# Two-layer graph network, one core: the second pass of layer 0 by lists for 16 blocks, more dense rounds and all own logits in layer 1, and row statistics by a sum and a square

## The chip, the cores and the metric

The kernel runs on one core of a Trainium2 chip. The metric is the device time of one execution in microseconds (us). All arithmetic on data is in float32.

The names of the engines in the profile: PE is TensorE (matrix products; PEld its weight loads), DVE is VectorE, ACT is ScalarE, POOL is GpSimd (here it issues the gathers), SP is SyncE (here it issues plain loads and stores). A letter q after a name is that engine's queue.

## The reference, cut to what matters

There are 3327 nodes with 512 features, and a sparse adjacency matrix with weights (some 0.3% of the entries, thick towards the first nodes, the "hubs", thin at the end, and with a full diagonal).

```
h  = relu(layernorm(x))
x  = x + adj @ (relu(adj @ (h @ W1) + b1) @ W2) + b2          # layer 0, hidden width 128

h  = relu(layernorm(x))                                       # layer 1
t  = adj @ h
attn_a = sigmoid([t, h] @ Wa.T + ba);  attn_b = sigmoid([t, h] @ Wb.T + bb)
scores[i, j] = s_left[i] + s_right[j]        # s_left, s_right: h @ W_sa times two halves of a_sa
e  = where(adj != 0, exp(-leaky_relu(scores, 0.01)), 0)
x_a = (e / (sum_j e + 1e-5)) @ (h @ W_sa)
x_b = t @ W_gcnb + b_gcnb
x  = x + sigmoid(attn_a * x_a + attn_b * x_b)
```

The layernorm has no weights; it divides by sqrt(variance + 1e-5).

## The kernel before

Nodes are padded to 3328 = 26 blocks of 128. The adjacency is given transposed, `adjT`. A *round* for a block of columns adds 128 (or two times 64) rows of some table, weighted by a piece of `adjT`. A round is *dense* where the rows are those of a known block, and goes *by list* where they are only the rows with an entry: for each group of 32 columns a list of rows is made in the kernel, and GpSimd gathers rows by it. `list_rooms` says how many list rounds of 64 rows a block's groups may take; if a group has more, a flag (`overflow`) sends the kernel through a full dense branch at its end.

**First pass of layer 0** (lines 540 to 595). Rows are normalized and multiplied with W1 (`u`), and all 26 blocks are summed densely for seven chunks of columns (`back`: 512 wide from the end, and one of 256), PE products L568. Beside it DVE takes the largest absolute value of each group (L572), from which `make_lists` makes the lists (`row_h`: node rows, `row_a`: adjacency pieces). GpSimd gathers the listed adjacency pieces into `ae` (`gather_adj`, L166), from the last blocks to the first; `gather_behind` takes one at a time and lets it wait for a product (`pace`). `load_own` loads a block's own diagonal pieces for blocks in `OWN`, whose first round is dense: the block itself, and so takes entries off the lists. Each chunk ends in `make_g`, whose rows go to `g_dram`.

**Second pass of layer 0** (L803 to L860). The chunks at the end, `LISTED = 2` of them (blocks 18 to 25), are summed by lists: `gather_g` gathers rows of g (24 in flight), `list_sums` adds them in small products (L784), one step for each block and a last one for the chunk's copy, and `gather_g` goes on as sums free its tiles. `SUMS` says beside which product a step stands. The other 18 blocks are `dense_chunks`, five rounds of 26 products (L825), whose loads go on SP's queue. Beside these, `make_h1` makes a chunk's rows: it loads x, adds b2 (L650), multiplies with W2 (px, L663), adds (L666), normalizes (`ln_relu`: bn_stats L234, bn_aggr L236, square root L238, Relu L244), scores the row (L623) and stores x and h. For a block outside `OWN` and `LATE` it also makes the row's *own logits* (`own_logits`, L630: the part `h @ Wa[d:]`, `h @ Wb[d:]` of the two attentions). `make_e_hub` and `add_hubs` do layer 1's first block, the hub, whose sums over all rows are dense (L709), as soon as rows are there. `next_late`, `next(hubs)` and `make_e_hub` are called from the loop over the products; the order on each engine is the order of these calls.

**Layer 1** (L903 to L1110). For the blocks 25 down to 1: `attend` gathers h rows by the list (or loads the block's own row into `h_own`), makes e in the other half of `ae`, and, for blocks in `OWN`, the own logits; `sums` multiplies (L981), `turn` transposes the sums (L995, copies L1010), `weigh` multiplies with W_gcnb and W_sa (L1035, L1042), `finish` makes the output. `segments` cuts a block's rounds into pieces of at most four. The three `LATE` blocks get their own logits at the beginning of the stage. `LEAD` and `pace` keep gathers three or four blocks ahead; `AE_PER = 2` adjacency pieces are gathered for each block.

## Time and profile before

| what | us |
|---|---|
| median of 14 executions | 838.49 (833.1 to 846.14) |
| the profiled execution | 841.48 |
| its span (first to last instruction) | 839.7 |
| PE busy | 744.0 (89%) |
| DVE busy | 507.2 (60%) |
| POOL busy | 460.8 (55%) |
| ACT busy | 194.4 (23%) |
| mean granted clock of PE | 0.937 |

How to read it: a busy time is a sum over a whole span in which different things bind in different stages, so shares by stage say more. The end of a matrix product is modelled in the trace, so a busy PE is not a PE at its peak. The granted clock is the share of full speed that PE was given. A gather shows as DMA_INDIRECT on POOL, and its idle time before is given with what ended it.

### The profile page before, as it was taken

How to read it: one execution, taken by the hardware profiler on the slowest of the kernel's cores; microseconds unless marked ns; L12 is line 12 of the kernel's file. 1: busy time of each engine (PE TensorE's matmuls, PEld its weight loads, DVE VectorE, ACT ScalarE, POOL GpSimd, SP SyncE). 2: the span in 40 equal slices, each digit the busy share in tenths (PEclk: the TensorE clock that was granted, in tenths of full speed). 3: DMA queues.
4: the chain of work that ended last, by engine and by line, in shares of the span. 5: the costliest groups of instructions: out<-in, count | busy, mean ns of one | idle time of the engine just before them, and what ended most of it. 6: DMA issues, size and time to landing. Idle time of an engine off the chain costs nothing.

```text
span 839.7 us, 11907 instructions
## 1 busy us (share of the span) xinstructions
PE 744.0 (89%) x3595; PEld 405.6 (48%) x3595; DVE 507.2 (60%) x1625; ACT 194.4 (23%) x402; POOL 460.8 (55%) x490
## 2 busy tenths in 40 slices
PE   9999799999897759698997759967999999999995
PEld 7774344344543324243463235643665655654454
DVE  7778868898760607788965134523666457453552
ACT  7770000000000105244542002211222222121112
POOL 2201756666557677525563766674556666767400
PEclk9999989999999769799998869986999999999999
DMA  8788989898696838789953755564668877767510
GB/s 274 241 287 262 332 242 282 249 278 276 186 290 220 276 98 307 224 275 319 330 179 114 238 139 155 181 192 122 193 200 249 252 212 222 236 204 230 171 51 29
DMA packets 104889, 185.08 MB, mean 220 GB/s; under 512 B 18401, under 2 KB 35441, under 8 KB 104818
## 3 DMA queue, kind: packets, MB, share of 16 engines
q1 hardware_dynamic: 66544, 113.43, 41.6%
q0 software_dynamic: 23264, 57.64, 24.8%
q10 hardware_dynamic: 15010, 13.18, 4.8%
q8 instruction: 30, 0.49, 0.2%
q14 instruction: 41, 0.34, 0.1%
HBM read 162.29 MB, written 22.26 MB: 220 GB/s over the span
## 4 chain that ended last, share of the span: by engine, by line
PE 74%; DVE 8%; issue 7%; DMA 4%; another core or an unknown queue 4%; ACT 1%; SPq 1%; POOL 0%; DVEq 0%; POOLq 0%; ACTq 0%
PE acc_u L568 15%; PE acc L981 13%; PE p_b L1035 12%; PE p_a L1042 11%; PE acc_g L825 8%; DMA xb<-in_x_dram 3%; PE pu L333 3%; PE ptt L995 3%; PE acc_hub L709 2%; DVE most L572 2%; PE px L663 2%; PE acc_s L784 1%; PE pt L325 1%; PE p_list L513 1%
## 5 line engine op out<-in xcount | busy, mean ns | idle before, releaser
L166 POOL DMA_INDIRECT ae<-in_adjT_dram,row_a x194 | 200.6, 1034 | 176.9 <-DVE past L519 54.2
L568 PE MATMUL acc_u<-a,rows 128*128 128x512 f32 (+1 forms) x364 | 162.7, 586 | 1.2 <-issue 1.0
L166 POOL DMA_INDIRECT hr<-h_rows,row_h x120 | 123.3, 1028 | 63.4 <-issue 28.4
L825 PE MATMUL acc_g<-a,g 128*128 128x512 f32 (+1 forms) x260 | 116.9, 584 | 9.2 <-DMA a<-in_adjT_dram 8.1
L572 DVE TENSOR_REDUCE most<-a 128x16 f32<-128x512 f32 (+1 forms) x182 | 112.7, 642 | 12.8 <-DMA a<-in_adjT_dram 8.7
L1035 PE MATMUL p_b<-W_g_sb,tyT 128*128 128x257 f32 x416 | 100.2, 393 | 14.6 <-DVE tyT L1010 13.7
L166 POOL DMA_INDIRECT rows<-h_rows,row_h x74 | 76.0, 1027 | 52.0 <-PE acc L981 21.4
L1035 PEld LDWEIGHTS p_b<-W_g_sb,tyT 128*128 128x128 f32 x416 | 78.2, 193 | 45.8 <-DVE tyT L1010 14.0
L568 PEld LDWEIGHTS acc_u<-a,rows 128*128 128x128 f32 x364 | 67.4, 197 | 60.5 <-issue 55.8
L1042 PE MATMUL p_a<-W_sa_sb,tyT 128*128 128x512 f32 (+2 forms) x216 | 93.5, 576 | 0.0
L1010 DVE COPY tyT<-ptt 128x512 f32<-128x512 f32 x51 | 34.8, 685 | 80.7 <-PE ptt L995 28.0
L825 PEld LDWEIGHTS acc_g<-a,g 128*128 128x128 f32 x260 | 50.4, 201 | 62.9 <-issue 49.8
L981 PE MATMUL acc<-hr,ae 64*64 64x512 f32 x480 | 69.3, 619 | 5.4 <-issue 4.9
L166 POOL DMA_INDIRECT g_row<-g_rows,row_h x48 | 49.2, 1025 | 23.7 <-issue 13.1
L1042 PEld LDWEIGHTS p_a<-W_sa_sb,tyT 128*128 128x128 f32 x216 | 40.9, 189 | 37.7 <-issue 35.9
L884 ACT ACTIVATE f<-f 128x2 f32<-128x2 f32 x26 | 5.3, 203 | 192.1 <-DVE f L883 98.1
L981 PEld LDWEIGHTS acc<-hr,ae 64*64 64x64 f32 x480 | 27.3, 138 | 36.8 <-issue 36.6
L343 ACT ACTIVATE gT<-acc_u,b_col 128x512 f32<-128x512 f32 (+1 forms) x7 | 4.6, 656 | 163.6 <-DMA a<-in_adjT_dram 91.3
L666 DVE TENSOR_TENSOR xb<-px,xb 128x512 f32<-128x512 f32 x26 | 17.3, 685 | 40.2 <-PE acc_g L825 21.4
L981 PE MATMUL acc<-rows,ae 64*64 64x512 f32 x296 | 39.3, 610 | 2.5 <-DVE ae L251 1.9
L623 DVE SCALAR_TENSOR_TENSOR junk<-rows,w_rows 128x512 bf16<-128x512 f32 x52 | 35.7, 687 | 6.3 <-ACT rows L244 3.1
L663 PE MATMUL px<-W_sb,sT 128*128 128x512 f32 x52 | 26.5, 643 | 13.3 <-issue 9.3
(159 smaller groups left out, 950.8 us busy)
## 6 DMA issues: line engine op xcount, KB each, us to landing
a<-in_adjT_dram SPq DMA_DIRECT2D x286, 256.0 KB
h_rows<-rows SPq DMA_DIRECT2D x26, 260.0 KB
x<-in_x_dram SPq DMA_DIRECT2D x26, 256.0 KB
xb<-in_x_dram SPq DMA_DIRECT2D x26, 256.0 KB
x<-xb ACTq DMA_DIRECT2D x26, 256.0 KB
x1b<-x SPq DMA_DIRECT2D x26, 256.0 KB
out_dram<-va SPq DMA_DIRECT2D x25, 256.0 KB
ae<-in_adjT_dram,row_a POOLq DMA_INDIRECT x194
```

Source lines behind the costliest of these rows:

```text
L166: return nc.gpsimd.indirect_dma_start(out=dst, out_offset=None, in_=table, in_offset=bass.IndirectOffsetOnAxis(ap=rows, axis=0), bounds_ch ...
L333: nc.tensor.matmul(pu[:, :HID], hT[:, k, :], W1_sb[:, k, :], start=(k == 0), stop=(k == KD - 1))
L568: added = nc.tensor.matmul(acc[:, :w], u[j], a[:, :w], start=(j == 0), stop=(j == NB - 1))
L572: nc.vector.tensor_reduce(most[:, : w // GW, j], a[:, :w].rearrange("p (b i) -> p b i", i=GW), axis=AX.X, op=ALU.max, apply_absolute_value ...
L623: return nc.vector.scalar_tensor_tensor(junk, h, 1.0, w_rows[:, s, :], op0=ALU.mult, op1=ALU.mult, accum_out=into)
L663: last_row[2] = nc.tensor.matmul(px, sT[:, b * P : (b + 1) * P], W2_sb, start=True, stop=True)
L825: added = nc.tensor.matmul(acc[:, :w], g[j], a[:, n % per, :], start=(n == 0), stop=(n == NB - 1))
L981: added = nc.tensor.matmul(taken[i]["acc"][h][q * HALF : (q + 1) * HALF, :], both[half_p, q * n + k, :], taken[i][k0][k][half_p, q, :D], s ...
L995: moved = nc.tensor.transpose(pt[:, k * P : (k + 1) * P], ty[h][:, k * P : (k + 1) * P], ident)
L1010: last = nc.vector.tensor_copy(dst, src)
L1035: nc.tensor.matmul(p_b[n][:, :WH], tyT[:, k, 0, :], W_g_sb[:, k, n * WH : (n + 1) * WH], start=(k == 0), stop=(k == KD - 1),)
L1042: last = nc.tensor.matmul(p_a[:, c0:c1], tyT[:, k, 1, :], W_sa_sb[:, k, c0:c1], start=(k == 0), stop=(k == KD - 1),)
```

## The change

- `LISTED` is 4: blocks 10 to 25 go by lists in the second pass; the dense chunks are 512, 512 and 256 columns wide. Gathers of g rows are thus 92 instead of 48.
- A tuple `TOP` of nine blocks gets a second dense round: rows 0 to 63 (for both halves of the block's columns), in layer 0 from `g_top`, in layer 1 from `h_top`. `OWN` now holds 19 blocks. `extra` is 0, 1 or 2, `list_rooms` is smaller (88 rooms in place of 97), and lists of `TOP` blocks leave out rows 0 to 63.
- The second pass is a loop over the three dense chunks, in which `SUMS` stand beside the second, and then a *free loop* of 35 turns without dense products. Its turns call list sums (`FREE_SUMS`), adjacency gathers (`FREE_AE`, behind the last g gather in GpSimd's order, and without `pace`), `next_late`, `add_behind` (a hub step if over five rows wait) and `make_e_hub`.
- All own logits are made in `attend`, from an own row that is loaded for every block; `w_own` and `bab_row` are loaded on SP's queue after layer 0; `LATE` is gone.
- `segments` leaves five rounds in one piece.
- In the second pass the addition of px also sums the row (`accum_out`), and ScalarE sums the squares of the centred row, in place of bn_stats and bn_aggr. The first pass keeps them.

The diff, cut to its core:

```diff
-LISTED = 2
+LISTED = 4
...
-LATE = 10, 11, 16
-OWN = 1, 6, 7, 8, 12, 13, 14, 15, 17, 18
+TOP = 2, 3, 4, 5, 9, 10, 11, 21, 24
+OWN = TOP + (1, 6, 7, 8, 12, 13, 14, 15, 17, 18)
 def list_rooms(n_blocks):
-    rooms = [0, 8, 7, 6, 5, 5] + 6 * [4]
-    return (rooms + n_blocks * [3])[:n_blocks]
+    rooms = [0, 8, 6, 5, 4, 4, 4, 4, 4] + n_blocks * [3]
+    rooms[21] = rooms[24] = 2
+    return rooms[:n_blocks]
...
-    extra = [int(i in OWN) for i in range(NB)]
+    extra = [int(i in OWN) + int(i in TOP) for i in range(NB)]
...
         r = rooms[i] + extra[i]
-        n = -(-r // SEG)
+        n = -(-r // SEG) - (r == SEG + 1)
...
+    def ln_relu_by_sum(dst, src, ln):
+        nc.vector.tensor_scalar(ln[:, 1:2], ln[:, 0:1], -1.0 / D, None, op0=ALU.mult)
+        nc.scalar.activation(dst, src, AF.Square, bias=ln[:, 1:2], accum_out=ln[:, 2:3])
+        nc.scalar.activation(ln[:, 3:4], ln[:, 2:3], AF.Sqrt, bias=eps, scale=1.0 / D)
+        nc.vector.reciprocal(ln[:, 4:5], ln[:, 3:4])
+        nc.vector.tensor_tensor(ln[:, 0:1], ln[:, 1:2], ln[:, 4:5], ALU.mult)
+        return nc.scalar.activation(dst, src, AF.Relu, bias=ln[:, 0:1], scale=ln[:, 4:5])
...
                 own = flag[:, groups, c0 // P + b]
                 nc.vector.tensor_tensor(own, own, apart, ALU.mult)
+                if extra[c0 // P + b] > 1:
+                    nc.vector.memset(flag[:HALF, groups, 0:1], 0.0)
...
-                    nc.vector.tensor_tensor(x1, px, x1, ALU.add)
+                    ln = l0w.tile([P, 5], F32, tag="ln5", name=f"ln_b{i}", bufs=3)
+                    nc.vector.scalar_tensor_tensor(
+                        x1, px, 1.0, x1, op0=ALU.mult, op1=ALU.add, accum_out=ln[:, 0:1]
+                    )
                     nc.scalar.dma_start(x1_dram[i], x1)
                     h = made_row(i)
-                    _, last_row[0] = ln_relu(h[:, :D], x1, l0w, f"b{i}")
+                    last_row[0] = ln_relu_by_sum(h[:, :D], x1, ln)
...
-                if not extra[i] and i not in LATE:
-                    own_logits(
-                        i, made_row(i),
-                        l0w.tile([P, D], BF16, tag="junk", name=f"junk_{i}", bufs=1),
-                    )
...
-                late.append(make_h1((c0, w), sT, False))
+                late.append(make_h1((c0, w), sT, c0 == ND))
...
-        SUMS = {1: (14, 16, 18, 20, 24), 2: (16, 18, 20, 22, 25)}
+        SUMS = 14, 16, 18, 20, 24
+        FREE_SUMS = 4, 5, 6, 7, 8, 18, 19, 20, 21, 22, 30, 31, 32, 33, 34
+        FREE_AE = {8: 6, 22: 6} | {n: 1 + n % 2 for n in range(23, 35)}
+        def add_behind():
+            if len(rows_made) - len(e_added) > 5:
+                next(hubs)
+        g_top = ae[1][:, : HID // GW, GW:]
+        for h in range(2):
+            nc.scalar.dma_start(
+                g_top[h * HALF : (h + 1) * HALF],
+                g_dram[:HALF, :].rearrange("j (k f) -> j k f", f=GW),
+            )
...
-                if n in SUMS.get(c, ()):
+                if c == 1 and n in SUMS:
                     next(summing)
-                elif c and n % 4:
-                    gather_behind(added)
-                if n % 2 or (c in (2, 3) and n % 4 == 2):
-                    with queued(last_e[0] if last and n < 8 else None):
-                        next_late()
-                if last and n >= NB - QUIET:
-                    continue
+                if n % per == per - 1 and n // per % 2:
+                    next_late()
                 if c > 1 and n % 3 == 2:
-                    next(hubs)
-                elif c > 1 and (n > 8 if last else n % 3 == 1):
-                    with queued(last_row[0] if last else None):
-                        make_e_hub()
+                    add_behind()
+                elif c > 1 and n % 3 == 1:
+                    make_e_hub()
...
+        for n in range(FREE_SUMS[-1] + 1):
+            if n in FREE_SUMS:
+                next(summing)
+            with queued(g_last[0]):
+                for _ in range(FREE_AE.get(n, 0)):
+                    next(columns)
+            next_late()
+            add_behind()
+            make_e_hub()
+        with queued(last_e[0]):
+            nc.scalar.activation(root, eps, AF.Sqrt)
         while late:
             next_late()
...
+    w_own = late_w.tile([P, 2, D], F32, tag="w_own", name="w_own")
+    nc.sync.dma_start(w_own, w_self.partition_broadcast(P))
...
+            if k0 == 0:
+                h_own = own_row(i)
             for k in range(n):
                 if k0 + k < extra[i]:
-                    h = spw.tile([P, ROW], F32, tag="h_own", name=f"h_own_{i}", bufs=3)
-                    nc.sync.dma_start(h, h_dram[i * P : (i + 1) * P, :])
+                    h = h_top if k else h_own
...
             if k0:
                 last = nc.vector.tensor_tensor(es, es, part, ALU.add)
-            elif extra[i]:
-                own_logits(i, hr[0][:, 0, :], spw.tile([P, D], BF16, tag="junk", name=f"junk_{i}"))
+            else:
+                own_of(i, h_own)
...
-        own_of(LATE[0], made[0])
+        own_of(0, own_row(0))
```

## The prediction

> **What bounds it now.** I read the slices first, then the groups by shape, then a table of busy time by stage, then the single instructions on GpSimd's queue, and last the chain. The slices show three stretches: TensorE (PE) near 9 up to slice 10 (first pass over the adjacency), broken digits from slice 11 to 23 (second pass), 9 from slice 28 on (layer 1).
>
> ```profile
> PE   9999799999897759698997759967999999999995
> DVE  7778868898760607788965134523666457453552
> POOL 2201756666557677525563766674556666767400
> PEclk9999989999999769799998869986999999999999
> ```
>
> The busy time by stage says the same in numbers. The stretches are the first dense round of the second pass (231 to 260 us), the second round (260 to 320), the third (320 to 374), the fourth (374 to 416), the fifth and narrow one (416 to 445), the last rows and the hub's end (445 to 474), the turn to layer 1 (474 to 494), and of layer 1 two pieces. Columns: PE, weight loads, DVE, ACT, POOL, granted clock, DMA share, GB/s.
>
> ```profile
> 231.00:260.00 29.00, 25.94 (x100) 11.38 (x98) 13.08 (x43) 0.47 (x1) 18.24 (x18) 1.00 0.94 309
> 260.00:320.00 60.00, 42.24 (x163) 16.94 (x164) 20.55 (x67) 8.92 (x20) 41.14 (x41) 0.77 0.58 174
> 320.00:374.00 54.00, 46.74 (x203) 20.79 (x203) 41.95 (x137) 20.18 (x36) 28.87 (x27) 0.91 0.84 273
> 374.00:416.00 42.00, 38.57 (x95) 17.12 (x94) 36.88 (x122) 21.28 (x34) 20.37 (x20) 1.00 0.97 323
> 416.00:445.00 29.00, 22.59 (x81) 14.62 (x81) 17.49 (x59) 11.15 (x21) 18.34 (x18) 0.98 0.57 181
> 445.00:474.00 29.00, 26.26 (x60) 11.43 (x64) 13.74 (x50) 6.65 (x17) 13.81 (x14) 0.91 0.62 209
> 474.00:494.00 20.00, 6.26 (x35) 2.65 (x28) 3.34 (x9) 1.70 (x4) 13.24 (x14) 0.60 0.47 128
> 556.00:580.00 24.00, 12.30 (x37) 4.98 (x36) 3.39 (x15) 1.64 (x4) 13.84 (x14) 0.58 0.50 136
> 580.00:700.00 120.00, 119.59 (x688) 72.64 (x684) 69.80 (x241) 28.80 (x62) 75.94 (x75) 1.00 0.74 217
> ```
>
> So layer 1 is PE's (119.6 of 120 us), and the second pass is nobody's: PE, DVE and DMA take turns, held together by waits. The chain that ended last names PE throughout, but with issue, DMA and unknown releasers of the second pass between:
>
> ```profile
> PE 74%; DVE 8%; issue 7%; DMA 4%; another core or an unknown queue 4%; ACT 1%; SPq 1%; POOL 0%; DVEq 0%; POOLq 0%; ACTq 0%
> ```
>
> Work taken out there moves the end only as far as the next chain allows. The likely next chain is GpSimd's queue, and its pace is in single instructions: 1.00 us each and 0.30 us to the next, so 1.30 us a gather.
>
> ```profile
> 257.77 1.00 POOL L166 DMA_INDIRECT g_row<-g_rows,row_h  x1 [0.30 <-issue]
> 259.07 1.00 POOL L166 DMA_INDIRECT g_row<-g_rows,row_h  x1 [0.30 <-issue]
> 260.37 0.99 POOL L166 DMA_INDIRECT g_row<-g_rows,row_h  x1 [0.30 <-issue]
> ```
>
> **The change, part by part.** *Lists for 16 blocks.* Two of the dense rounds go (columns 1280 to 2303): 2 x 26 products of two instructions, 104 x 0.43 us (the spacing: 40 in 17.4 us) = 45 us of PE, and 52 loads of 256 KB = 13.6 MB, 44 us at the 309 GB/s of the first round. The sums of blocks 10 to 17 by lists come in: 8 blocks of 4 or 5 rounds, 8 instructions each, in tiles that overlap (30 in 1.0 us): 9 us at most. Gathers of g rows rise from 48 to 92. The room table falls from 97 to 88 rooms, so gathers of adjacency pieces and of h rows fall from 194 to 176 each; all gathers together go from 436 to 444. I counted the non-empty rows of each group of 32 columns in the reference's inputs: no block exceeds its new room, so the fallback branch stays shut.
>
> When does layer 0 end? I follow the gathers. (a) Up to the second round's end (319.9 us, its copy out of PSUM) the order is the same but for 13 adjacency gathers fewer; I take 316 (305 to 322). (b) The third round has 256 columns: 52 products at 0.235 us (14 in 3.29 us) = 12.2, and three px pairs (2.6) and some hub products: 16 us, 332. (c) Four turns of the free loop, 2 us each (half a row on DVE, below): the sums of blocks 18 to 21 start at 340. (d) Each sum frees the rows for the next gathers. Still to come are 22 for blocks 14 to 17, 6 adjacency gathers, 24 for blocks 10 to 13 (46 of the 92 were issued in (a), two of them for block 14): 52 x 1.30 = 67.6, and 2.3 us for the last to land (572.8 issued, 574.9 landed, elsewhere in this trace): 410. (e) From the last sum to the turned sT took 4.4 us (368.3 to 372.7): 414.5. (f) The last rows: 445.4 to the last h store at 454.7 is 9.3 us for two rows; now four, and a further one costs DVE 0.77 + 0.46 + 0.77 = 2.0 us before its store: 13.3, so 428. (g) From the last h store to layer 1's first product took 19.0 us (473.7). w_own's 512 KB and the first own logits (1.5 us of DVE before the turn's copies) stand in that path now (1.7 us at 309 GB/s, and 1.5): 22 (19 to 25), so 450 against 473.7. **Layer 0 gives 23.7 us.** DVE and PE lie beside this: between 340 and 410 PE has some 50 us of work (35 hub pairs and 13 px pairs at 0.86, 9 of sums); DVE has 13 rows at 4.45 = 58 us. If this cover fails, the second pass is bound by DVE at about the same place.
>
> *Means by the addition, variances by ScalarE.* A second-pass row loses bn_stats and its aggregation (0.684 + 0.166) on DVE and gains an accumulator read (0.08, the row of the scores) and one small operation (0.15): 0.62 us less. ACT gains one 128x512 pass, which no row shows in this form; Relu of the same shape is 0.806, a copy 0.58, so between these and 1.0 with a read. The latency of a row stays (0.69 + 0.17 against 0.08 + 0.15 + 0.8), so this is worth nothing on the gathers' chain and 26 x 0.62 = 16 us where DVE bounds. DVE per row is then 0.69 + 0.77 + 0.46 + 2 x 0.77 + 4 x 0.287 = 4.6, or 4.45 where accumulator reads overlap.
>
> ```profile
> L234 DVE BATCH_NORM_STATS2 bn_b<-xb 128x6 f32<-128x512 f32 x26 | 17.0, 684 | 0.1
> L244 ACT ACTIVATE rows<-xb,ln_b 128x512 f32<-128x512 f32 x26 | 20.2, 806 | 9.1 <-PE acc_hub L709 5.6 <-DVE ln_b L240 2.1 <-issue 1.3
> L238 ACT ACT_TABLE_LOAD x8 | 10.3, 1283 | 21.6 <-DVE ln_b L236 16.7 <-DMA x<-xb 3.5 <-issue 1.4
> ```
>
> The table loads are few (8 and 10) and last 1.28 us. [...]
>
> *Own logits in layer 1.* 13 blocks' pairs (2 x 0.77 + 0.16 = 1.7 us) leave DVE's second pass (22 us, worth nothing on the gathers' chain) and go to layer 1, whose DVE is at 69.8 of 120 us: 1.7 us more in a turn of some 11 us. Blocks 17 to 12 have them there already, and PE has no idle time in those turns. Nothing, then; without that cover 13 x 1.7 = 22 us. The row that they read comes by 15 or so more loads of 260 KB on SP, at a DMA share of 0.74. The 36 more loads of own pieces (16 KB) are on ACT's queue, which has nothing else at the chunks' ends.
>
> *More dense rounds.* Rooms and extra rounds together go from 107 to 116. A fourth round lengthens PE's part of a turn from 2.63 to 3.49 us (22 against 30 products in the chain), 0.87 us: 9 x 0.87 = **7.8 us more** in layer 1, all on the path. POOL has 216 gathers there now (120 + 74 of h rows, 22 of adjacency) and 222 then (176, and the 46 that some 100 in the first pass and 30 in the free loop leave): nothing.
>
> Sum: 839.7 - 23.7 + 7.8 = 823.8 of span, with 1.8 around it 825.6. The profiled execution (841.5) is 3.0 above the median, so 838.5 - 15.9 = 822.6; I say **823**, for the case itself 811 to 835.
>
> **Rivals.** *The gaps close too* (797). PE lost 13.7 us at 474 to 494 and 11.7 at 556 to 580, both in half clock. The sum keeps them. If shifted gathers break them up, and the free loop starts at 325, it is 823 - 25 - 1 = 797. Against: the order of these gathers is hardly changed.
>
> *GpSimd's unbroken runs stop PE* (862, slower). Wherever POOL issued gathers without a break for over 13 us, PE stood or crawled until the run's end: 242 to 272 (PE's gap 270 to 278), 290 to 313 (297 to 316), 430 to 444 (439 to 446), 462 to 489 (479 to 493), 543 to 574 (556 to 577). It lost 12 to 14 us in each of 23 to 31. The free loop makes runs of 28 (36 us) and, as the later adjacency gathers no longer wait for a product, of up to 48 (62 us). If PE loses 16 of the first, the second starts 8 later; 30 of the second delay the last sums by 31: 823 + 39 = 862. It decides once the last sums come 16 us after 410. Against: runs of 8 between 580 and 740 leave PE at 1.00 clock, and POOL may merely have run on while PE waited for something else.
>
> *Nothing gained* (839). The free loop has no dense products to bridge waits. Its PE work of some 50 us at the clock of 474 to 494 (0.60) needs 83, which puts the last sums at 423 or later and the rest slower: +16. [...]
>
> *Lists overflow*: then everything is done again, beyond 1,500 us; the count above excludes it.
>
> **How the numbers follow.** Forecast 0.46, gaps close 0.24, nothing gained 0.12, runs stop PE 0.18. A measurement here tells 0.3% (2.5 us) from no change. Faster takes the first two and a third of the third: 0.74; same 0.08; slower 0.18. The range leaves out half of the slow case and the far part of the fast one: 796 to 848.
>
> **What would show it.** Right: the products of acc_g fall from 260 to 156 instructions; h's last store near 428, first product of layer 1 near 450; GpSimd at 1.30 us without long pauses between 340 and 410; layer 1 longer by 8. Wrong: PE digits of 5 or less with clock 0.5 through the free loop while POOL is unbroken; ACT_TABLE_LOAD in the dozens; gaps before the tyT copies in layer 1 where own logits precede them.

## The result and the profile after

The kernel after takes 905.4 us (median of 10) where the kernel before takes 840.4 (47 runs): 1.076 times as long, interval 1.071 to 1.080. The forecast was 823, in a range of 796 to 848. The profiled execution took 907.9 us, with a span of 906.2. Ratios, here and below, compare only executions in the faster of two states that a kernel's executions show, so they can differ a little from the quotient of the medians.

The slices of after, for comparison with those of before: PE, VectorE, GpSimd, and the clock granted to PE.

```profile
PE   9999989888878788674656628996999989999995
DVE  7779788887613245142426515652665563646643
POOL 3203666666670623676730474675766776765500
PEclk9999999999997889576766959995999999999999
```

Between slices 16 and 23, counted from 0 (362 to 544 us), PE is at 2 to 7 with a clock of 5 to 9, while POOL is mostly at 6 or 7. That comes near the sign that the prediction named for "wrong" (PE digits of 5 or less at half clock, POOL unbroken). The table by stage (us, PE, weight loads, DVE, ACT, POOL, clock, DMA share, GB/s): first dense round, second, third, then the free loop and the last rows in pieces.

```profile
231.00:275.00 44.00, 32.17 (x106) 12.46 (x104) 14.24 (x46) 0.47 (x1) 28.93 (x28) 0.88 0.72 208
275.00:326.00 51.00, 40.17 (x171) 17.88 (x171) 15.01 (x54) 12.13 (x28) 20.29 (x20) 0.83 0.74 233
326.00:347.00 21.00, 21.00 (x71) 14.13 (x72) 15.05 (x58) 11.14 (x24) 0.00 (x0) 0.92 0.73 242
347.00:380.00 33.00, 21.54 (x135) 9.15 (x134) 5.54 (x21) 8.11 (x15) 20.02 (x20) 0.70 0.32 86
380.00:415.00 35.00, 27.46 (x156) 12.37 (x155) 15.45 (x60) 11.96 (x25) 25.71 (x25) 0.74 0.48 134
415.00:445.00 30.00, 15.52 (x68) 6.86 (x66) 12.46 (x48) 12.05 (x25) 21.58 (x22) 0.78 0.43 127
445.00:475.00 30.00, 16.52 (x120) 7.42 (x119) 5.28 (x21) 3.47 (x8) 13.93 (x14) 0.59 0.13 34
```

Nobody is busy throughout from 347 on: PE at 52 to 78% (at a clock of 0.59 to 0.78, which stretches its busy time: in before the large matmuls follow 0.43 us apart at a clock of 1.00, from 240.7 to 258.1 us, and 0.85 apart at 0.50, from 278 to 283), DVE at 17 to 44%, the DMA nearly empty at the end (0.13). What PE waits for in that stretch stands in its groups between 347 and 472 us (out<-in, partitions x elements, count | busy, mean ns | idle before and what ended it):

```profile
L784 PE MATMUL acc_s<-g_row,ae 64*32 64x128 f32 x280 | 26.5, 332 | 19.3 <-issue 17.0 <-DMA g_row<-g_rows,row_h 1.0 <-DMA ae<-in_adjT_dram,row_a 0.9
L784 PE MATMUL acc_s<-g,ae 64*32 64x128 f32 x72 | 9.4, 348 | 7.0 <-issue 6.9
```

"issue" is time in which the engine waited for nothing that the profile shows. The second group needs no gathered row at all, and idles like the first. The single instructions around 364 us show how it goes: PE's list sums come in bursts 0.7 or 1.4 us apart, beside gathers that follow at 1.30 us.

```profile
363.61 0.37 PE L784 MATMUL acc_s<-g,ae 64*32 64x128 f32 x1 [0.78 <-issue]
363.63 0.62 PE L784 MATMUL acc_s<-ae,ae 64*32 64x128 f32 x3
365.07 0.69 PE L784 MATMUL acc_s<-ae,ae 64*32 64x128 f32 x5 [0.82 <-issue]
```

GpSimd's queue in the same microseconds:

```profile
362.81 1.00 POOL L164 DMA_INDIRECT g_row<-g_rows,row_h  x1 [0.30 <-issue]
364.11 1.00 POOL L164 DMA_INDIRECT g_row<-g_rows,row_h  x1 [0.30 <-issue]
365.41 0.99 POOL L164 DMA_INDIRECT g_row<-g_rows,row_h  x1 [0.30 <-issue]
```

By events, before and after: first dense round's copy out of PSUM 260.1 and 275.5, second 319.9 and 325.8; the third ends at 346.9; last list sum 472; last h store 454.7 and 506.0; layer 1's first product 473.7 and 525.2; end 839.7 and 906.2. So 51.5 us are lost ahead of layer 1 and 15.0 in it. The theory to test was the prediction's rival that unbroken runs of gathers stop PE; I call a stretch like the one above a **crawl**.

The trace of before has one too, beside the run of gathers from 290 to 313 us that the prediction names for this rival: there PE's list sums stand in the same steps of 1.4 us.

```profile
300.14 0.53 PE L784 MATMUL acc_s<-g_row,ae 64*32 64x128 f32 x4 [1.01 <-issue]
301.56 1.10 PE L784 MATMUL acc_s<-g_row,ae 64*32 64x128 f32 x4 [0.90 <-issue]
```

But the prediction's "wherever" goes too far: beside the 13 gathers from 316 to 334 us PE was busy for 17.9 of 18 us, at a clock of 0.96.

### The profile page after: what moved, and what is told of

Its sections match the earlier page's. It is cut to its first block, busy times and chain, and to the rows that moved or that the text cites. A ratio compares the mean times of both kernels' runs of the same rounds, so it can differ in the third digit from the quotient of the medians.

```text
span 906.2 us, 12320 instructions
## 1 busy us (share of the span) xinstructions
PE 757.7 (84%) x3815; PEld 411.8 (45%) x3815; DVE 491.6 (54%) x1637; ACT 211.5 (23%) x449; POOL 473.7 (52%) x507
## 4 chain that ended last, share of the span: by engine, by line
PE 67%; issue 18%; POOL 6%; DMA 3%; DVE 3%; ACT 2%; POOLq 0%; another core or an unknown queue 0%; SPq 0%; DVEq 0%; ACTq 0%
PE acc_u L579 15%; PE acc L1020 13%; PE p_b L1074 11%; PE p_a L1081 10%; POOL g_row L164 4%; PE acc_g L836 4%; PE ptt L1034 3%; PE pu L340 3%; DMA a<-in_adjT_dram 2%; PE px L665 2%; PE acc_hub L709 1%; PE acc_s L784 1%; PE pt L332 1%; PE p_list L524 1%; POOL ae L164 1%
## 5 line engine op out<-in xcount | busy, mean ns | idle before, releaser
L164 POOL DMA_INDIRECT ae<-in_adjT_dram,row_a x176 | 183.6, 1043 | 128.3 <-DVE past L530 53.5
L164 POOL DMA_INDIRECT hr<-h_rows,row_h x112 | 115.0, 1027 | 58.9 <-issue 28.5
L164 POOL DMA_INDIRECT g_row<-g_rows,row_h x92 | 95.1, 1033 | 91.2 <-PE acc_s L784 53.9
L1074 PE MATMUL p_b<-W_g_sb,tyT 128*128 128x257 f32 x416 | 104.3, 400 | 19.7 <-issue 18.6
L583 DVE TENSOR_REDUCE most<-a 128x16 f32<-128x512 f32 (+1 forms) x182 | 113.2, 643 | 13.3 <-DMA a<-in_adjT_dram 8.8
L164 POOL DMA_INDIRECT rows<-h_rows,row_h x64 | 67.6, 1056 | 88.4 <-DVE e_hub L258 46.3
L669 DVE SCALAR_TENSOR_TENSOR xb<-px,xb 128x512 f32<-128x512 f32 x26 | 17.9, 691 | 105.6 <-PE px L665 64.8
L836 PE MATMUL acc_g<-a,g 128*128 128x512 f32 (+1 forms) x156 | 67.5, 570 | 5.4 <-DMA a<-in_adjT_dram 3.9
L1020 PE MATMUL acc<-hr,ae 64*64 64x512 f32 x448 | 59.9, 607 | 1.9 <-issue 1.6
L1081 PEld LDWEIGHTS p_a<-W_sa_sb,tyT 128*128 128x128 f32 x216 | 41.1, 191 | 39.5 <-issue 36.1
L784 PE MATMUL acc_s<-g_row,ae 64*32 64x128 f32 x368 | 32.9, 325 | 23.9 <-issue 21.6
L836 PEld LDWEIGHTS acc_g<-a,g 128*128 128x128 f32 x156 | 30.0, 202 | 34.1 <-issue 22.5
L665 PE MATMUL px<-W_sb,sT 128*128 128x512 f32 x52 | 36.0, 829 | 11.3 <-ACT sT L854 6.1
```

What stands on the lines that cost most here:

```text
L164: return nc.gpsimd.indirect_dma_start(out=dst, out_offset=None, in_=table, in_offset=bass.IndirectOffsetOnAxis(ap=rows, axis=0), bounds_ch ...
L583: nc.vector.tensor_reduce(most[:, : w // GW, j], a[:, :w].rearrange("p (b i) -> p b i", i=GW), axis=AX.X, op=ALU.max, apply_absolute_value ...
L665: last_row[2] = nc.tensor.matmul(px, sT[:, b * P : (b + 1) * P], W2_sb, start=True, stop=True)
L784: nc.tensor.matmul(acc[part, b * P : (b + 1) * P], ae[i][half_p, 2 * k0 + q * (k1 - k0) + kk - k0, :GW], t[half_p, :], start=(kk == 0), st ...
L836: nc.tensor.matmul(acc[:, :w], g[j], a[:, n % per, :], start=(n == 0), stop=(n == NB - 1))
L1020: added = nc.tensor.matmul(taken[i]["acc"][h][q * HALF : (q + 1) * HALF, :], both[half_p, q * n + k, :], taken[i][k0][k][half_p, q, :D], s ...
```

## The experiments

Of six chips drawn for the experiments, two gave the kernel before 734 to 735 us and four 825 to 839, near the 838 to 840 of the case's own runs. Each result below is given beside the kernel before on its own chip.

**1. The free loop without GpSimd** (chip: before 830.6).

```
+    by_sync = [False]           # True from the start of the free loop to its last stored row
     def gather(dst, table, rows, last):
+        if by_sync[0]:
+            return nc.sync.dma_start(dst, table[:P, :])
         return nc.gpsimd.indirect_dma_start(
...
```

> The kernel after, but the gathers of the free loop (g rows and adjacency pieces) are plain loads of 128 fixed rows on SP's queue: the wrong rows, and no work for GpSimd between the third dense round's end and the last row. Its sums are wrong, the instructions on TensorE, VectorE and ScalarE the same. Theory 'runs stop TensorE': the last list sum, 465 us in the profile of after, comes near 405 (third round's end 347, then some 50 us of TensorE work), layer 1's first product near 460 instead of 525, the whole near 845. Rival 'the free loop is short of work that can run, TensorE waits for rows and sums': last sum no earlier than 450, the whole within 890 to 905.

Measured: 826.1 us, 0.996 of before (0.992 to 1.000). Last list sum at 402.5, layer 1's first product at 455.1. The prediction had 410 and 450 for these two in a loop in which gathers cost PE nothing. The table by stage shows PE at work throughout:

```profile
347.00:380.00 33.00, 32.44 (x298) 16.57 (x297) 19.70 (x72) 20.33 (x39) 2.00 (x2) 1.00 0.56 173
380.00:400.00 20.00, 17.23 (x101) 7.54 (x103) 15.12 (x59) 16.25 (x30) 0.00 (x0) 0.91 0.69 199
```

49.7 us of PE in 53, against 21.5 of 33 in the same window of after. With GpSimd's gathers, layer 1's first product came 70 us later (525.2, on another chip). This doesn't say yet whether they cost that by their pace or by holding PE up; experiment 14 divides it.

**2. The rows' statistics alone, put into before** (same chip). The new function and the addition's sum, nothing else of the change.

> The kernel before with the means from the addition and the variances by ScalarE's squares, nothing else. Theory 'worth nothing': within 0.5% of before (840), since the second pass is not VectorE's. Rival 'it saves VectorE's 16 us where rows bound (320 to 416 us)': 826 to 834. Rival 'ScalarE's square lengthens each row's chain (0.8 us and table loads of 1.28 us)': 846 or more.

Measured: 842.5, 1.019 of before (1.013 to 1.024): slower by 1.3 to 2.4%, as the second rival had it. Experiment 12 takes this up again.

**3. After without the second extra dense round** (same chip).

```
-TOP = 2, 3, 4, 5, 9, 10, 11, 21, 24
+TOP = ()
...
-    rooms = [0, 8, 6, 5, 4, 4, 4, 4, 4] + n_blocks * [3]
-    rooms[21] = rooms[24] = 2
-    return rooms[:n_blocks]
+    rooms = [0, 8, 7, 6, 5, 5] + 6 * [4]
+    return (rooms + n_blocks * [3])[:n_blocks]
```

> The kernel after with the room table of before and one dense round for the ten blocks that had one: 97 rooms and 10 extra rounds instead of 88 and 28. Theory of the prediction (0.87 us on TensorE for each of nine rounds in layer 1): 8 us less in layer 1, and some gathers more (194 instead of 176 of adjacency pieces) in the second pass; by 'runs stop TensorE' these cost up to 10 us there, so 895 to 908 in all. Rival 'the extra dense rounds are what made the change slow' (their list flags and own pieces in the first dense round, their products in layer 1): below 875.

Measured: 931.2, 1.122 of before (1.116 to 1.128). Neither theory: without them it is slower by 4% (after is at 1.076, on another chip). Layer 1 takes 411.8 us instead of 381.0. From 15 us ahead of the last h store on, GpSimd has 257 gathers to make instead of 221: 131 adjacency pieces are fetched ahead of that in both, so the longer lists leave 18 pieces and 18 row gathers more for layer 1. In layer 1 GpSimd then makes five unbroken runs of 20 to 26 gathers, where after makes one (24, at 595 us). That these runs bring the loss by crawls is likely and not shown.

**4. Products beside gathers, first attempt** (same chip). A kernel of PE products and gathers alone.

> This kernel leaves the whole computation out. TensorE runs twelve stretches of 200 steps without a wait between them: six with one 128x512 f32 product a step (0.86 us as in the kernel before), six with four products of 64 rows, 32 columns of weights and 128 elements. At step 40 of each stretch another engine starts 32 pieces of work: gathers of 128 B pieces, of 512 B rows, of 2 KB rows, of 512 B rows with a memset of 256 elements between any two, GpSimd memsets of 512 elements without a gather, and 32 plain loads of 256 KB on SP's queue. Theory 'runs stop TensorE': in the three stretches with unbroken gathers at 1.30 us the spacing of products rises from 0.86 us to 1.4 or more from about the tenth gather on, and comes back within 3 us of the last; with memsets between the gathers it stays nearer 0.86, and with memsets alone or SP's loads it is 0.86. Rival 'GpSimd merely ran on while TensorE waited': 0.86 in all six, and one spacing in the six short ones.

Measured: most gathers didn't stay in their stretches but were issued ahead, back to back, in the first 320 us. There PE made 24 or 25 matmuls in 10 us beside gathers of 128 B pieces (10 to 38 us), and 4 to 6 beside gathers of longer rows (40 to 90). That looked like a matter of size, and a refill of PE's instructions (16 KB, each 256 instructions, on a DMA queue of its own) lay at 39.3 us. So the next kernel held the gathers in place and tried both.

**5. Size, refill and breaks** (chip: before 839.1).

> This kernel leaves the whole computation out. TensorE runs 12 stretches of 192 128x512 f32 products (four instructions each) without a wait; in each, GpSimd starts one row of work, in its order: 40 unbroken gathers of 128 B pieces, of 512 B rows, of 2 KB rows; 16 of 512 B placed between two of the 16 KB instruction refills that the profile shows every 256 TensorE instructions; 16 across such a refill; 40 of 512 B with a memset of one element after each, with one after every fourth, with a memset of 512 after every fourth, after every eighth, with a memset of 256 after each; 100 memsets alone; and 40 plain loads on SP's queue. Theory 'a refill in an unbroken run of gathers leaves TensorE without instructions until the run's end': in the three stretches of 40 the spacing of products goes from 0.86 us to 5 (as 40 to 92 us of the first such kernel) from some 20 to 100 instructions after the refill to the end of the run, whatever the row's size; the 16 between refills cost nothing, the 16 across one some 5 us; with breaks the spacing stays 0.86 where the break is long enough, and memsets and SP's loads alone cost nothing. Rival 'it is the rows' size': 128 B pieces cost nothing even across a refill, and the 16 between refills cost as much per gather as the 40.

Measured, as time lost by PE while the run lasted: 40 unbroken gathers cost 10.7 us with 128 B pieces, 11.9 with 512 B rows, 10.7 with 2 KB rows; 16 gathers cost 0.4, across a refill or not. A memset of one element after each gather changes nothing (13.4). A memset of 512 elements (0.53 us) after every fourth takes it all away (0.2), after every eighth part of it (3.8), one of 256 after each all (0.1). 100 memsets or 40 plain loads on SP's queue cost nothing. So size is out. In the three unbroken runs the crawl began 38 to 40 us after the run's start, and the refill lay 12 us in: that left the refill open. The first unbroken run (from 77.8 us) and the one with 512 elements after every fourth (from 1308.3 us); columns PE, weight loads, DVE, POOL, clock, DMA share, GB/s:

```profile
77.00:130.00 53.00, 44.42 (x99) 18.71 (x97) 0.00 (x0) 40.05 (x40) 0.92 0.09 13
1308.00:1364.00 56.00, 56.00 (x132) 24.77 (x131) 0.00 (x0) 45.05 (x50) 1.00 0.18 46
```

**6. Where it starts** (chip: before 825.3).

> This kernel leaves the whole computation out, as the one with the instruction refills did. Three stretches of 192 products with a run of 64 unbroken gathers of 512 B rows that starts 8, 58 and 33 products after a refill (64 products apart); then three of 384 steps of four small products each (14 us from refill to refill) with 40 gathers: unbroken, with a memset of 512 elements after every fourth, with one of 128 after every second; at last 64 unbroken gathers with 500 copies of 64 elements each on VectorE and ScalarE. Theory 'a refill does not come into force during an unbroken run': the crawl starts some 105 to 125 TensorE instructions after the first refill in the run, so 74, 31 and 52 us into the first three runs (the refills lie 48, 5 and 27 us in), and within 20 us of the start with the small products. Rival 'the run's length alone, 38 us': 38 us into all of them. If every engine that fetches instructions is held up, VectorE and ScalarE have gaps over 2 us as well; if TensorE alone is, they have none.

Measured: with 128x512 products 42.6, 39.5 and 40.4 us into the run, though the first of these runs has no refill ahead of its crawl and the others have one 3 and 24 us in: the refill theory falls. With small products it is 9 us. In table form (columns as in the tables by stage), the first of the large runs (from 44.9 us) and the small one (from 709.2 us), each split where it turns:

```profile
40.00:85.00 45.00, 45.00 (x107) 19.89 (x106) 0.00 (x0) 0.00 (x0) 31.00 (x31) 1.00 0.17 44
85.00:130.00 45.00, 17.87 (x23) 5.37 (x22) 0.00 (x0) 0.00 (x0) 33.11 (x34) 0.58 0.20 50
700.00:718.00 18.00, 18.00 (x167) 17.64 (x166) 0.00 (x0) 0.00 (x0) 6.99 (x7) 1.00 0.09 23
718.00:761.00 43.00, 12.70 (x45) 5.20 (x43) 0.00 (x0) 0.00 (x0) 32.94 (x33) 0.53 0.20 51
```

107 matmuls in 45 us become 23 in the next 45; 167 in 18 us become 45 in 43. From the run's start to the crawl it is 92 to 99 matmuls (with their weight loads some 184 to 198 instructions) in one case and 82 (164) in the other: counted in instructions the two come near each other, and in time they don't. So neither length nor refill sets it alone; it is as if the engines lived on a **stock of instructions** while gathers run. With PE idle, copies on VectorE and ScalarE crawl too, from 18 us into the run, at 0.7 and 1.4 us apart. It isn't PE's own trouble. The two later runs with rests among small products can't be set beside the unbroken one: there PE stood at half clock (0.50) from the start.

**7 and 8. Rests in the kernels, first attempt** (same chip).

```
+        if breaking[0] and gathers[0] % 4 == 0:
+            rest = nc.gpsimd.memset(idle, 0.0)     # after: 512 elements, 0.53 us; before: 448, 0.48 us
+        gathers[0] += 1
...
```

> The kernel after, with one GpSimd memset of 512 elements (0.53 us) ahead of every fourth gather, from the start until block 15 of layer 1. Theory 'unbroken runs stop TensorE': layer 0 gets back most of what e1 showed without gathers (last list sum 465 to some 410; 54 gathers cost 13 x 0.55 = 7 us more), layer 1's first product near 462, and the whole 820 to 845 instead of 905. Rival 'the stall is from the gathers themselves, broken or not': 895 or more.

> The kernel before with the same memsets ahead of every fourth gather. Theory 'unbroken runs stop TensorE': the gaps of before at 270 to 278, 296 to 317, 439 to 446, 479 to 493 and 556 to 577 go, in all some 40 to 60 us of which half lies on the path: 800 to 820. Rival 'these gaps of before are other waits': 838 to 850.

Measured: 898.1, 1.074 (1.067 to 1.082) for after; 825.2, 0.998 (0.995 to 1.002) for before. Inconclusive: nothing held a memset behind the gather ahead of it, and in the traces unbroken runs of up to 24 gathers (after) and 17 (before) stand with the memsets elsewhere.

**9. How long a rest must be** (chip: before 838.3).

> This kernel leaves the whole computation out. The kernel before it showed the crawl 39 to 43 us into a run with 128x512 products (some 180 TensorE instructions), 9 us with small ones (some 165) and 18 us with VectorE's and ScalarE's copies (some 80 and 65), wherever the refills lay. Theory 'while gathers follow at 1.30 us the engines share a stock of some 150 to 250 instructions, and a rest of GpSimd of some 0.5 us gives back about 25 to 30 of it': with VectorE's copies alone (4.4 a us) the crawl starts 35 us or later into the run, with products and VectorE's copies together (9 instructions a us) near 20; two runs of 25 gathers with one, two and five memsets of 512 between them crawl some 6, 12 and 25 us later than an unbroken run of 50 would; with a rest after every second gather, products with both engines' copies (13 a us) keep up for most of the run, after every fourth they don't; small products (18 a us) keep up with a rest after every gather and not after every second. Rival 'each engine has its own': VectorE's copies alone crawl at 18 us, with products beside them at 18 too, and the products at 39.

Measured, start of the crawl: PE's large products alone 40 us into the run; VectorE's copies alone 27; ScalarE's alone 20; with products and VectorE's copies together, VectorE at 17 and PE at 33. Neither theory as stated: engines do draw each other down, but not as one common count. In two runs of 25 gathers with one memset between them the crawl begins at 40 us, with two at 42, with five (2.6 us) not before 64, near the run's end. So a rest of 0.5 us gives back little and one of 2.6 us most of it: the second run of 25 then crawls some 28 us after its own start, where a fresh run goes on for 40. With a rest after every second gather, products and both engines' copies keep up for the whole run; after every fourth ScalarE crawls from 17 us on, VectorE from 21 and PE from 37. Small products keep up with a rest after each gather, and with one after every second for 28 us. PE, in the run with one memset (from 677.1 us) and in the one with five:

```profile
677.00:717.00 40.00, 40.00 (x94) 17.48 (x92) 0.00 (x0) 0.00 (x0) 30.94 (x32) 1.00 0.18 48
717.00:742.00 25.00, 8.96 (x10) 2.67 (x10) 0.00 (x0) 0.00 (x0) 19.21 (x20) 0.59 0.20 52
1055.00:1120.00 65.00, 64.84 (x152) 28.57 (x151) 0.00 (x0) 0.00 (x0) 49.80 (x53) 1.00 0.18 47
```

**10 and 11. Rests that stay in place** (same chip): ahead of every second gather, from the start until block 15 of layer 1.

```
+        if breaking[0] and gathers[0] % 2 == 0:
+            with queued(latest[0]):                # behind the last gather
+                rest = nc.gpsimd.memset(idle, 0.0)
...
```

> The kernel after with a memset of 512 elements ahead of every second gather, now held in place by the order (in the earlier kernel with breaks the profile shows runs of 20 to 25 gathers at 1.29 us with no memset among them). From the start until block 15 of layer 1. Theory 'a stock used up during runs': the crawls at 352 to 384 and 396 to 465 us go, gathers take some 1.6 us each, so that the last list sum stands near 425 to 440 and the whole at 845 to 875 where after is 905. Rival 'the gathers themselves hold the engines up, whatever lies between them': 900 or more.

> The kernel before with the same rests ahead of every second gather. Theory 'a stock used up during runs': the gaps at 270 to 278, 297 to 317, 439 to 446, 479 to 493 and 556 to 577 go or shrink, the first pass is unchanged, POOL has 0.27 us more a gather: 805 to 825 where before is 838 to 840. Rival 'these gaps are ordinary waits': 838 or more.

Measured: after 839.3, 1.003 of before (0.999 to 1.006), where without rests it is at 1.076; before 805.4, 0.963 (0.958 to 0.968). This is the verdict on cause: work was added, and both kernels got faster (before on this very chip; after by its ratio, as it wasn't run without rests here). Before with rests, by slices:

```profile
PE   8999979998899978889998989988599999999995
POOL 2300888888868888888788888887647666676400
PEclk9999999999999999999999999998599999999999
```

POOL is busier than in before from slice 4 to 28 (counted from 0), and PE's broken digits of the second pass are gone (none under 7 in slices 11 to 23); what is left at slice 28 comes right where the rests end, in a run of 22 gathers. On these chips it is the fastest version found. But the change still costs 34 us between two kernels with the same rests. In the two profiled executions (30.9 us apart) 18.6 of it lie ahead of layer 1's first product (459.8 against 441.2) and 12.3 in layer 1.

**12. The parts, with rests until block 11** (chip: before 735.0).

> The kernel before with a memset of 512 elements ahead of every second gather, as in the run that gave 805, but on until block 11 of layer 1 instead of 15. There the profile still shows one turn of 28.6 us among turns of 12, in a run of 22 gathers right after the rests end. Theory 'a stock used up during runs': that turn comes to some 12, so 785 to 797. Rival 'this turn is long for another reason': 802 to 808.

> The kernel after with rests on until block 11. With rests until 15 one turn of 40 us stands among turns of 12 (839 in all). Theory 'a stock used up': 808 to 820, still slower than the kernel before with the same rests, since the free loop's 54 gathers now take 1.57 us each and the rows after the last sum 52 us to layer 1. Rival: 835 to 842. If the change's own saving (23.7 less 7.8, as predicted) were there once the stalls are gone, it would be some 775.

> The kernel after with rests until block 11, and with the second pass's means and variances from VectorE's bn_stats again, as before; lists, room table and own logits as in after. Theory 'ScalarE's squares and table loads (16 of 1.28 us) lengthen the rows after the last sum, 32 us to the last store against the 17.7 predicted': at least 8 us less than the run with rests alone. Rival 'worth nothing either way': within 3 us of it. Rival 'VectorE's 16 us come back': 5 to 16 us more.

> The kernel before with rests until block 11 and the rows' means from the addition, variances by ScalarE. Alone, without rests, this part cost 1.9%. Theory 'it lengthens a row's chain by ScalarE's square and the switch of tables': 5 to 15 us more than the run with rests alone. Rival 'it cost only by shifting GpSimd's runs against TensorE's work': within 3 us. Theory of the prediction, where rows bind VectorE: up to 16 us less.

Measured: 762.5 (1.037; 1.034 to 1.040), 783.1 (1.066; 1.062 to 1.070), 780.9 (1.064; 1.060 to 1.067), 765.5 (1.042; 1.038 to 1.046). All expectations were made for a chip like the earlier ones, and this one is different: rests only cost here. Whether rests until block 11 take the last long turn away on a chip that crawls stays untested. In the first kernel, after the rests end, 60 gathers follow at 1.30 us (575 to 654 us), and PE doesn't notice:

```profile
575.00:655.00 80.00, 80.00 (x479) 48.01 (x478) 49.83 (x176) 20.05 (x45) 61.56 (x61) 1.00 0.85 257
```

By the earlier chips' measure (9 to 40 us) this run should have crawled for half its length. So the crawl is no law of the program: it depends on the chip, or on something else that differed from one draw to the next. The difference of the first two kernels is the change's own: 20.5 us more. Their traces divide it: layer 1's first product comes at 430.1 and 443.5, 13.4 us later, and layer 1 is 6.9 us longer (330.3 and 337.2). The rows' statistics by sum and square cost 3.0 us in one pair (executions of 759.6 to 763.5 against 762.9 to 768.9) and 2.1 in the other, where the executions overlap: a small loss at most, and no gain. The 1.9% of experiment 2 belong to a chip that crawls, and were not traced to a place.

**13. The own logits alone, put into before** (chip: before 839.1).

> The kernel before with all own logits computed in layer 1, from a stored row loaded there, as in the change; the vector w_own stays loaded early. Theory of the prediction 'worth nothing': within 0.5% of before. Rival 'VectorE's 22 us in the second pass come off': 818 to 825 where before is 838. Rival 'the loads or the longer VectorE turn delay layer 1': 13 x 1.7 = up to 22 us more.

Measured: 835.1, 0.994 of before (0.991 to 0.998): 4 to 5 us less, near nothing.

**14. After itself, on a chip without the crawl** (before 734.4).

> The kernel after, unchanged, beside the kernel before. The last four runs were on a chip where before takes 735 us and where 60 gathers without a rest leave TensorE at full clock; the others on four chips where it takes 825 to 839. On a chip of the first kind this shows the change without any crawl: by the prediction's own sum (-15.9) 719; by the theory that the rows after the last sum and the free loop's gathers cost more than forecast (with rests on both, the change cost 20.5 us there) 735 to 755. On a chip of the second kind: 1.07 to 1.09 times before, again.

> The kernel before with rests until block 11, again. On a chip where before takes 735: 1.037 times before, as measured. On a chip where it takes 825 to 839: theory 'a stock used up during runs': 785 to 797, below the 805 with rests until block 15, since the turn of 28.6 us goes; rival: 802 or more, since the rests make GpSimd the bound of layer 1's turns (8 gathers at 1.57 = 12.5 us against TensorE's 10.8 to 11.7).

Measured: after 754.8, 1.029 (1.025 to 1.033); before with long rests 763.9, 1.041 (1.037 to 1.045). So without any crawl the change costs 20.4 us. The free loop of after there, PE's groups from 297 to 378 us, against the same group shown above:

```profile
L784 PE MATMUL acc_s<-g_row,ae 64*32 64x128 f32 x280 | 20.0, 313 | 14.8 <-DMA g_row<-g_rows,row_h 14.7
```

The "issue" is gone: the sums wait for their rows' gathers, and these follow at 1.34 us. GpSimd's queue is the bound, as the prediction had it (POOL made 21 and 45 gathers in these 29 and 60 us):

```profile
301.00:330.00 29.00, 24.57 (x239) 12.29 (x239) 17.54 (x70) 17.99 (x34) 21.98 (x21) 0.93 0.69 208
330.00:390.00 60.00, 43.43 (x239) 19.07 (x239) 26.84 (x104) 25.54 (x54) 46.60 (x45) 0.76 0.47 133
```

From the third dense round's end to layer 1's first product after took 178.3 us in its own profile, 107.0 in experiment 1 and 130.6 here. So of the 71 us that GpSimd's gathers cost there, some 24 are their pace and some 48 the crawl, as far as three chips can be compared.

## Why the prediction was wrong, by its steps

- **Sum and sign.** -15.9 forecast; +65 on the case's own chip, which crawls, +20.4 on one that doesn't. Neither is a gain, and both lie beyond the range (at most +9.5 against 838.5). The mechanism that decides on the first kind was a rival at 0.18 and 862; it was priced at 39 us, with 16 from the first run of gathers. By the division above the crawl cost some 48 between the third round and layer 1 alone.
- **"DVE and PE lie beside this"** is the step that failed. PE's work was sized well (some 50 us forecast, 49.7 in experiment 1), but it doesn't lie beside gathers where they crawl: the last g row was issued at 429, and the last sum ended at 472, where the forecast had the sums follow 2.3 us behind the gathers. Against the rival I put that runs of 8 leave PE at full clock in layer 1. That was true, and no counter-evidence: 8 gathers last 10.4 us, and PE's crawl began 9 to 40 us into a run (experiments 6 and 9), by what the engines issued.
- **(a) 316, (b) 16 us, (c) 340.** 325.8, 21.1 us, and the first sum of the free loop at 349. The first dense round ended 15 us later than before's, with PE's weight loads held up by 0.7 to 2.5 us beside the gathers from 254 to 268. The profile puts these waits down to loads of `a`, so a crawl is likely there and not shown; with rests (experiment 10) that round's copy stands at 260.6 instead of 275.5.
- **(d) 52 gathers at 1.30, 67.6 us.** 54 gathers. Where nothing crawls they took 72.4 us (301.9 to 374.3), so the term was right to 7%; on the profiled chip 78 (352.1 to 430).
- **(e) 4.4 and (f) 13.3.** 11.5 and 22.3 after; 8.8 and 22.1 in experiment 14, so most of it isn't the crawl. This is the step that failed where nothing crawls: 13 us more than forecast. The working allowed for four rows behind the last sum. In experiment 14 six additions of rows come after it (385 to 404 us), and 44 of the 104 hub instructions, 19 us at 0.43. The last sum is sooner and layer 1 isn't.
- **(g) 22.** 19.2, and 18.7 in experiment 14: at the low end of 19 to 25. The 3 us added for w_own and the own logits don't show (19.0 in before).
- **What the two rounds gave** was read off a stretch (320 to 445 us, 125.5 from copy to copy) that the crawl had already stretched: with rests it took 118.0 on a chip that crawls (296.1 to 414.1, experiment 11) and 118.9 on one that doesn't (281.7 to 400.6, experiment 12). On a chip without the crawl the kernel before is 105 us faster; there is less to gain there, and 44 more gathers x 1.34 = 59 us of GpSimd's queue stand against 45 us of PE. There is no trace of before without rests on such a chip. With rests on both, layer 0 lost 13.4 us where 23.7 were to be gained.
- **More dense rounds, 7.8 us on the path.** Turns of 10.8 and 11.7 us stand side by side in experiment 14, so 0.87 a round is right, and where nothing crawls layer 1 is 6.9 us longer (experiment 12). But the step asked only PE: experiment 3 shows that on a chip that crawls the kernel is 4% slower without these rounds; the gathers that they spare GpSimd in layer 1 are the likely reason. The count of 222 gathers from there on was right (221), and "nothing" for them wasn't tried against the table without them.
- **Means and variances, nothing.** VectorE's busy time fell by 15.6 us (16 forecast), which gained nothing: 2 to 3 us lost in experiment 12, and 1.9% in experiment 2, on a chip that crawls. ScalarE's square takes 0.72 and its read 0.19, within the bounds of 0.58 and 1.0. There are 16 table loads in the whole kernel (20 in before), not the dozens that the prediction named as a sign of "wrong"; the six ahead of the rows' square roots stand here:

```profile
L250 ACT ACTIVATE rows<-xb,ln_b 128x512 f32<-128x512 f32 x26 | 18.7, 720 | 66.2 <-DVE ln_b L249 54.3 <-DVE ln_b L252 5.9 <-issue 2.5
L251 ACT ACT_TABLE_LOAD x6 | 7.7, 1283 | 0.1
```

- **Own logits, nothing.** 4 to 5 us less alone (experiment 13).
- **"Nothing gained", by a low clock in the free loop**: the clock was 0.59 to 0.78 there, where this rival took 0.60. But a low clock doesn't make such gaps. In experiment 6 the clock was 1.00 beside the same gathers ahead of the crawl (40 to 85 and 700 to 718 us) and 0.58 and 0.53 in it, and large matmuls in a crawl follow 2.8 us apart (351.60 and 354.41 in experiment 9), where at half clock alone, as in before from 278 to 283 us (0.50), they are 0.85 apart. Nor does the clock just follow the gaps: after that crawl the small products of experiment 6 kept PE busy for 230 of 230 us (770 to 1000), and the clock stayed at 0.50.

What the stock is stays open: no run here shows it.

## What to carry to other kernels

Where an engine idles on "issue" in steps of 0.7 and 1.4 us beside gathers at an even pace, don't take a time read from there as the cost of the work: first give GpSimd's queue rests (0.5 us after every second gather here) and look again, and do so on more than one chip: where nothing crawled, the rests cost 3.7 to 4.1%. A change that trades dense work for gathers pays GpSimd for each (1.30 to 1.34 us here), and work that counts as "beside" them has to be seen running beside them. When a chain is cut short, count what is still queued behind its end (six rows here, not four).

## What the runs showed of the hardware

- Beside back-to-back gathers, PE came down to steps of 0.7 to 2.8 us between instructions after some 9 to 40 us, on four of the six chips drawn; copies on VectorE and ScalarE came down too, after some 17 to 27 us (experiments 6 and 9; 0.7 and 1.4 us apart in 6); 2.6 us without a gather gave back most of what a run had used up (28 us to the next crawl instead of 40); plain loads on SP's queue (40 in 26 us) and GpSimd's memsets (100) did nothing of the kind.
- The size of the gathered rows (128 B to 2 KB) had no part in it (40 gathers cost PE 10.7, 11.9 and 10.7 us).
- Two chips of six showed none of it: 60 gathers in 79 us with PE at full clock on one, and on both the kernel before in 735 us instead of 825 to 839.
- A throttled clock did not come back while small products (64 rows, 32 columns) kept PE busy: 0.50 from 720 us to the end of PE's work at 2567 (experiment 6). The same products had run at 1.00 ahead of the crawl (700 to 718 us).
